# A graph kernel's third pass over the adjacency: resident rows moved to its end, two loads moved ahead of a branch, four sends moved to another queue

## The chip, the cores and the metric

The kernel is one launch on one core of a Trainium2 chip. The metric is the device time of the launch in microseconds (us). Three runs of the kernel before gave 1063.72, 1066.23 and 1070.17 us, a median of 1066.23. The profile is of another execution, which took 1063.12 us; its trace spans 1061.4 us from the first to the last instruction, and 1.7 us lie around that.

Names used below: TensorE (PE; its weight loads are shown as PEld), VectorE (DVE), ScalarE (ACT), GpSimd (POOL) and SyncE (SP). A name with a "q" behind it (SPq, ACTq) is the engine's sequencer, which issues DMAs, reads registers and branches.

## The reference

There are N = 2708 nodes with D = 128 features; `adj` is a sparse random matrix with weights, 2708 x 2708, of which the kernel gets the transpose as `adjT`. Four graph layers follow each other, each as `x = layernorm(x + layer(x, adj))`. The change lies in the second one:

```python
XW = jnp.matmul(X, W)
s_col = jnp.matmul(XW, a[0, :f])
s_row = jnp.matmul(XW, a[0, f:])
Z1 = jax.nn.leaky_relu(s_row[:, None] + s_col[None, :], negative_slope=0.01)
den = jnp.exp(Z1)
num = jnp.matmul(A, den)
att = jnp.where(num != 0, den / jnp.where(num != 0, num, 1.0), 0.0)
H = jnp.matmul(A, jnp.matmul(att, XW))
```

`num` would be a product of two full matrices. The kernel avoids that. `exp(leaky_relu(r + c))` is one of two products, `exp(r)exp(c)` or `exp(0.01r)exp(0.01c)`, depending on the sign of `r + c`. So for columns of `den` sorted by `c`, going from one block of columns to the next changes few rows' choice, and `num` of a block is `num` of the block before it plus the contribution of few rows of `adjT`.

## The kernel before

**The whole, in order of time.** A first pass over `adjT` makes the degrees and the first product of layer 0 (its last products start at 150 us). Then a search finds each node's four nearest nodes, and a second pass over `adjT` (`by_panels`, line 189, called at 1010) makes layer 0's output. The third pass, the subject here, runs from 442.4 us to 499.1 us of the trace. The loop over 44 steps (`block_layer`, line 1604) follows until about 724 us. Then three more passes by panels end layer 1 and make layers 2 and 3 (`two_layers`, line 1695).

**The third pass** (lines 1308 to 1447) does two things side by side.

The first is a product. `lc` holds for each node 22 weights: for each of the 11 chains of blocks, two sums are started (for the two forms of the exponential). `add_line(i, h, src)` (line 1335) multiplies row tile `i` of `adjT` (128 rows), half `h` of its 2708 columns (1354 columns), by `lc[:, i, :]`. Since only 32 columns of weights are used, it is four products side by side, one per quarter of the half row, each into 32 partitions of one PSUM bank, `banks[h]`. There are 21 full row tiles and one of 20 rows. Tiles 0 to 15 have to be loaded again: 32 half rows of 693,248 bytes, which `lines` (line 1022) lists, half 0 first; `line(n)` (line 1412) does the next n of them. Tiles 16 to 20 lie on the chip, in `res`, since the first pass: `own_line(n)` (line 1421) does the next n of these 10 half rows. `add_last_rows(h)` adds the 20 last rows. When a half's rows are all added, `end_half(h)` (line 1354) has ACT copy `banks[h]` to `heads` and ACT's queue send `heads` in four DMAs to the tile `carry`, which holds the two starting sums of each block.

The half rows are loaded by `load_line` (line 1033) on SP's queue into 11 places, `berths`: six in `ring`, three in `more`, two in `y_place`. The first 11 are loaded ahead. Each place is used again: `follows` (line 1026) says which half row is loaded when another has been read, and `line` issues that load. Half row 20 goes to the place of 11, 21 to that of 12, up to 28 to that of 19; then 29, 30 and 31 go to the places of 24, 25 and 26. Half rows 20 to 23 lie in the four places that are, put together, the first two thirds of `ring`.

The second thing is a sort, in between. It makes the order of the columns (`in_rank_order`, four parts, `ranks_known`), and then for each block the list of up to 126 rows to be fetched (`in_list_order`, four parts). Behind these come the row numbers `slot_i` and the weights `lw` (`listed`; six groups of `weights`, of which DVE makes four and ACT two).

What order TensorE, VectorE and ScalarE do all of this in is written out by hand, as the list `turns` (line 1429). SP and POOL take their instructions in the order in which the scheduler of the build puts them. On SP that is, behind the loads: three loads of the 20 last rows into `res` (line 1441), a read of `flag` into a register (line 1512), the branch (line 1773), the loop's carry rows.

**The branch** (line 1773) chooses between the loop by blocks and a dense way out, by the largest count in a list. Each engine reads `flag` and branches for itself.

**The loop** (line 1652) takes blocks two by two: 22 steps for each half of the columns. `load(i)` (line 1494) fetches for step i, per block, up to 126 half rows by an indirect DMA of POOL, and on SP two rows of `carry` into partitions 126 and 127 of the same place (line 1505). It uses one of three places in `ring`; step 0's is half row 20's and 21's, step 1's is half row 22's and 23's, step 2's is that of half rows 29 and 30. `find_num` multiplies by `lw`, `find_inv` has ACT do a logarithm and an exponential, `mix_1` to `mix_3` are DVE's. `keep(i)` sends two rows of the error term of each of the step's blocks on SP to `carry` for a later block. `add(i)` multiplies by `xws` into `hacc`. Loads run two steps ahead: `load(0)` and `load(1)` stand first behind the branch (lines 1647 and 1648), `load(i + 2)` first in step i.

Of the kernel before, what the change touches and what calls it, by code (L numbers as in the profile page):

```python
# [16 lines left out]
P = 128  # L17
# [4 lines left out]
KC = 126  # L22
CH = 4
# [29 lines left out]
def kernel(  # L53
# [999 lines left out]

    with tc.tile_pool(name="rank", bufs=1) as rank:
# [297 lines left out]
        HEADS = 96  # L1352

        def end_half(h):

            if not carries:
                carries.append(big.tile([P, NQ * P], F32, tag="y", name="carry"))
            tot = heads[:, h * span : (h + 1) * span]
            nc.scalar.copy(tot[:, : edges[4] - edges[3]], banks[h][:, : edges[4] - edges[3]])
            nc.scalar.copy(tot[:64, edges[4] - edges[3] :], banks[h][:64, edges[4] - edges[3] : span])  # L1360
            for g in range(4):
                w = edges[g + 1] - edges[g]
                nc.scalar.dma_start(
                    carries[0][HEADS : HEADS + 2 * NCH, h * HALF + edges[g] : h * HALF + edges[g + 1]],
                    tot[32 * g : 32 * g + 2 * NCH, :w],
                )
# [45 lines left out]
        def line(n):  # L1412
            for _ in range(n):
                at = loaded[0]
                loaded[0] += 1
                i, h = lines[at]
                add_line(i, h, line_at(at), last=at == 2 * S - 1)
                if at in follows:
                    load_line(follows[at])

        def own_line(n):
            for _ in range(n):
                h, i = divmod(held[0], FULL - S)
                held[0] += 1
                add_line(S + i, h, res[:, i, h * HALF : (h + 1) * HALF], last=held[0] == FULL - S)
# [4 lines left out]
            (line, 4), (blocks_of_edges,), (line, 7), (own_line, 2), (last_xw,), (in_rank_order, 0), (line, 2),  # L1430
            (in_rank_order, 1), (line, 2), (in_rank_order, 2), (count_lone,), (line, 2), (counts,), (line, 1),
            (add_last_rows, 0), (own_line, 3), (line, 2), (ranks_known,), (line, 1), (own_line, 1), (in_list_order, 0),
            (line, 1), (in_list_order, 1), (in_list_order, 2), (line, 1), (own_line, 1), (in_list_order, 3),
            (line, 1), (add_last_rows, 1), (next_weights,), (own_line, 1), (next_weights,), (line, 1), (next_weights,),
            (own_line, 1), (next_weights,), (line, 1), (next_weights,), (own_line, 1), (line, 1), (next_weights,),
            (line, 5),
# [3 lines left out]
        for c in range(C):  # L1440
            nc.sync.dma_start(res[few(c), FULL - S, cols[c]], adjT[FULL * P :, cols[c]])
# [3 lines left out]
        xws, lw = work["xws"], work["lw"]  # L1445
        order.close()
# [35 lines left out]
    adj_half = adjT.rearrange("n (h k) -> (n h) k", h=2)  # L1482
# [3 lines left out]

    def block(s):

        return s % NCH * CH + s // NCH

    steps = [(h, q) for h in range(2) for q in range(NQ)]
    rows = {}

    def load(i):
        h, q = steps[i]
        rows[i] = strip(i).rearrange("p (n k) -> p n k", n=2)
        for n in range(2):
            nc.gpsimd.indirect_dma_start(  # L1498
                out=rows[i][:KC, n, :], out_offset=None, in_=adj_half[:, :],
                in_offset=bass.IndirectOffsetOnAxis(ap=slot_i[h][:KC, 2 * q + n : 2 * q + n + 1], axis=0),  # L1500
                bounds_check=2 * N - 1, oob_is_err=False,
            )
            b = block(2 * q + n)
            at = 2 * b if b % CH else HEADS + b // CH * 2
            nc.sync.dma_start(rows[i][KC : KC + 2, n, :], carry[at : at + 2, h * HALF : (h + 1) * HALF])
# [98 lines left out]
    def block_layer():  # L1604
        with (
# [40 lines left out]
            with tc.manual_schedule(engines={e.engine for e in engines}):  # L1646
                load(0)
                load(1)
# [166 lines left out]
```

## Time and profile before

| stretch of the trace, us | what | PE busy | granted PE clock | DMA engines' busy share |
|---|---|---|---|---|
| 442.4 to 490.8 | third pass, half rows 0 to 29 | 47.30 of 48.40 | 0.99 | 0.84 |
| 490.8 to 499.1 | third pass, half rows 30 and 31 | 2.25 of 8.30 | 0.75 | 0.81 |
| 499.1 to 505.7 | to the loop's first logarithm | 3.66 of 6.60 | 0.53 | 0.30 |
| 505.7 to 519.0 | the loop's first steps | 10.33 of 13.30 | 1.00 | 0.49 |
| 519.0 to 723.8 | the rest of the loop | 204.09 of 204.80 | 1.00 | 0.55 |
| 0 to 1061.4 | the trace; the execution took 1063.12 | 984.6 (93%) | 0.97 | |

Each row gives PE's busy time in a stretch, the share of full speed that its clock was granted and how busy the 16 DMA engines were. Where PE's busy time equals the stretch, PE is what sets the pace; where it falls short, something else ends PE's waits. In such a profile a wait is put down to the event that came last before the waiting instruction began. Where the view names SP's line 1811 for a wait of PE, the two only ended at the same moment; what ended both is worked out below.

### The profile page before, as it was taken

Reading aid. Unit: us, or ns where it says so; the run is one execution under the profiler, and the core shown is the slowest. Engines: PE = TensorE matmul, PEld = TensorE weight load, DVE = VectorE, ACT = ScalarE, POOL = GpSimd, SP = SyncE. Lnnn points to the kernel's source line nnn. Section 1 sums busy time; section 2 is a strip of 40 time slices with the busy share of each in tenths; the row PEclk is TensorE's granted clock in tenths of the full one; section 3 lists DMA queues with packets and bytes.
Section 4 is the critical chain, followed back from the end, with each engine's and each line's share of the span. In section 5 each row is a group of like instructions: output and inputs, shape, how many; then the busy total and the mean of one; then the engine's idle time right before and its main releaser. Section 6 shows DMA issues by size and latency. Waiting matters only on the chain.

```text
span 1061.4 us, 11655 instructions
## 1 busy us (share of the span) xinstructions
PE 984.6 (93%) x3773; PEld 482.9 (45%) x3773; DVE 637.0 (60%) x1358; ACT 331.5 (31%) x609; POOL 275.1 (26%) x339
## 2 busy tenths in 40 slices
PE   0898999999998998796899999999999999999996
PEld 0346544444444556562333333334445544564444
DVE  5985438999944577862899999994121121222222
ACT  0000126555501245402767776762010100010000
POOL 4000000000477673023788534430121100000000
PEclk9989999999998998698999999999999999999998
DMA  9999340000185666696455555556665957484652
GB/s 339 373 342 270 109 157 1 0 1 1 32 279 183 221 182 201 224 359 200 118 167 152 149 146 157 142 163 215 219 193 169 308 168 219 145 276 149 227 170 72
DMA packets 102001, 191.00 MB, mean 180 GB/s; under 512 B 14022, under 2 KB 43342, under 8 KB 101930
## 3 DMA queue, kind: packets, MB, share of 16 engines
q1 hardware_dynamic: 83764, 152.22, 43.5%
q0 software_dynamic: 17728, 37.62, 12.8%
q8 instruction: 32, 0.52, 0.2%
q10 hardware_dynamic: 438, 0.31, 0.1%
q14 instruction: 39, 0.32, 0.1%
HBM read 214.80 MB, written 4.16 MB: 206 GB/s over the span
## 4 chain that ended last, share of the span: by engine, by line
PE 48%; DMA 1%; DVE 1%; ACT 1%; issue 1%; POOL 0%; POOLq 0%; DVEq 0%
PE acc L204 28%; PE num L1619 9%; PE hacc L1477 9%; PE mis L285 1%; DMA ring<-carry 1%; DMA ring<-in_adjT,slot_i 0%; PE mis L1750 0%; DVE inv L1466 0%; DVE err L1462 0%; ACT gb L234 0%; PE mis L1716 0%; DVE inv L1469 0%; PE mis L1746 0%; ACT inv L1452 0%; POOL rstd L253 0%
## 5 line engine op out<-in xcount | busy, mean ns | idle before, releaser
L1498 POOL DMA_INDIRECT ring<-in_adjT,slot_i x88 | 104.4, 1187 | 95.9 <-PE num L1619 67.0
L1619 PE MATMUL num<-ring,lw 128*64 128x512 f32 (+1 forms) x528 | 113.7, 557 | 6.1 <-DMA ring<-carry 3.8
L1477 PE MATMUL hacc<-inv,xws 128*128 128x512 f32 (+1 forms) x264 | 111.7, 559 | 0.6 <-ACT inv L1455 0.3
L699 PE MATMUL acc<-zT,z 128*128 128x512 f32 (+2 forms) x252 | 102.2, 552 | 0.0
L1452 ACT ACTIVATE inv<-num,plain 128x1024 f32<-128x1024 f32 x88 | 80.6, 916 | 57.6 <-PE num L1619 41.4
L253 POOL TENSOR_TENSOR rstd<-rstd,minus_half 128x4 f32<-128x4 f32 (+1 forms) x18 | 17.3, 960 | 313.5 <-DVE rstd L252 313.5
L234 ACT COPY gb<-acc 128x512 f32<-128x512 f32 (+2 forms) x18 | 9.6, 535 | 251.1 <-PE acc L204 251.1
L1462 DVE TENSOR_TENSOR err<-inv,num 128x1024 f32<-128x1024 f32 x88 | 74.6, 856 | 21.0 <-ACT inv L1455 19.7
L700 ACT COPY key<-acc 128x512 f32<-128x512 f32 (+2 forms) x126 | 67.1, 535 | 55.1 <-issue 27.9
L204 PE MATMUL acc<-ring,y 128*128 128x512 f32 (+2 forms) x192 | 82.0, 558 | 0.5 <-issue 0.5
L1477 PEld LDWEIGHTS hacc<-inv,xws 128*128 128x128 f32 x264 | 46.5, 189 | 77.6 <-issue 34.2
L729 POOL DMA_INDIRECT got<-y_rows,where x66 | 71.5, 1083 | 26.6 <-DVE near_sum L742 8.9
L204 PE MATMUL acc<-ring,xs 128*128 128x512 f32 (+2 forms) x192 | 78.1, 550 | 0.0
L1469 DVE SCALAR_TENSOR_TENSOR inv<-gb,g_inv,inv 128x1024 f32<-128x1024 f32 x88 | 77.2, 917 | 0.1
L204 PE MATMUL acc<-ring,carry 128*128 128x512 f32 (+2 forms) x192 | 74.5, 542 | 0.0
L204 PE MATMUL acc<-ring,m_rows 128*128 128x512 f32 (+2 forms) x192 | 74.3, 542 | 0.0
L1466 DVE SCALAR_TENSOR_TENSOR inv<-err,inv 128x1024 f32<-128x1024 f32 x88 | 72.3, 861 | 0.1
L575 POOL TENSOR_TENSOR slot_e<-near,sim 128x44 f32<-128x44 f32 (+2 forms) x3 | 0.7, 241 | 267.3 <-DVE d2inv L603 265.2
L699 PEld LDWEIGHTS acc<-zT,z 128*128 128x128 f32 x252 | 45.8, 190 | 50.4 <-issue 45.0
L1455 ACT ACTIVATE inv<-inv 128x1024 f32<-128x1024 f32 x88 | 67.6, 768 | 2.8
L1619 PEld LDWEIGHTS num<-ring,lw 128*64 128x64 f32 x528 | 37.4, 138 | 65.0 <-issue 47.5
L701 DVE MAX8 near<-key 128x8 f32<-128x2708 f32 x21 | 62.3, 2965 | 2.7 <-ACT key L700 2.7
(376 smaller groups left out, 1370.0 us busy)
## 6 DMA issues: line engine op xcount, KB each, us to landing
ring<-in_adjT SPq DMA_DIRECT2D x74, 1024.0 KB
ring<-in_adjT SPq DMA_DIRECT2D x20, 677.0 KB
ring<-in_adjT SPq DMA_DIRECT2D x17, 768.0 KB
part<-in_adjT SPq DMA_DIRECT2D x12, 1024.0 KB
ring<-in_adjT SPq DMA_DIRECT2D x17, 552.0 KB
more<-in_adjT SPq DMA_DIRECT2D x10, 677.0 KB
res<-in_adjT SPq DMA_DIRECT2D x4, 1280.0 KB
part<-in_adjT SPq DMA_DIRECT2D x3, 768.0 KB
```

Of the source, the lines that this page charges most:

```text
L204: nc.tensor.matmul(accs[c][: lhsT.shape[-1], :w], lhsT=lhsT, rhs=src, start=start, stop=stop)
L699: nc.tensor.matmul(pks[c][:p, : cw[c]], lhsT=z2[:, :p], rhs=zT[:, cs], start=False, stop=True)
L700: nc.scalar.copy(key[:p, cs], pks[c][:p, : cw[c]])
L729: nc.gpsimd.indirect_dma_start(out=got[:p, :], out_offset=None, in_=y2_rows[:, :], in_offset=bass.IndirectOffsetOnAxis(ap=where[:p, t, k : ...
L1452: nc.scalar.activation(inv, num[:, :w], AF.Ln, scale=plain[:, 0:1], bias=plain[:, 1:2])
L1455: nc.scalar.activation(inv, inv, AF.Exp, scale=-1.0)
L1462: nc.vector.tensor_mul(err, inv, num[:, :w])
L1466: nc.vector.scalar_tensor_tensor(inv, err, 2.0, inv, op0=ALU.subtract, op1=ALU.mult)
L1469: nc.vector.scalar_tensor_tensor(inv, gb[:, col : col + w], g_inv[:, q : q + 1], inv, op0=ALU.max, op1=ALU.mult)
L1477: nc.tensor.matmul(haccs[:, o:e], lhsT=xws[:, q, :], rhs=inv[:, o:e], start=(q == 0), stop=(q == NQ - 1))
L1498: nc.gpsimd.indirect_dma_start(out=rows[i][:KC, n, :], out_offset=None, in_=adj_half[:, :], in_offset=bass.IndirectOffsetOnAxis(ap=slot_i[ ...
L1619: nc.tensor.matmul(num[n * (BJ + 2) : (n + 1) * (BJ + 2), o:e], lhsT=lw[:, 2 * q + n, :], rhs=rows[i][:, n, c0 + o : c0 + e], start=True, ...
```

## The change

It consists of four edits.

1. `turns` is written anew. Most `own_line` steps move back: before, they came as 2, 3, 1, 1, 1, 1, 1; now as 4, 1, 1, 1, 1, 2, the last two being the end of the list. `line` steps move forward in turn; the `add_last_rows(1)` goes from the middle to just before the last two own lines. The accumulation of each half now ends with an own line (`last` in `own_line`) and no longer with the last loaded half row.
2. `load` and what it needs (`block`, `steps`, `rows`, `adj_half`, `HEADS`) are defined before the third pass, and `load(0)` and `load(1)` are called at its end. Their DMAs thus stand before the read of `flag` and the branch on POOL (four indirect DMAs) and on SP (four carry row DMAs, ahead of the sends below).
3. `end_half` sends only half 0 on ACT's queue. Half 1's four sends are issued on SP by `send_half`, behind the carry rows.
4. The loads of the 20 last rows (line 1441) stand behind these sends.

In the built kernels the same numbers of matmuls, DMAs and vector operations stand on the engines; SP has four sends more and ACT four fewer.

```diff
+    def load(i):
+        h, q = steps[i]
+        rows[i] = strip(i).rearrange("p (n k) -> p n k", n=2)
+        for n in range(2):
+            nc.gpsimd.indirect_dma_start(
+                out=rows[i][:KC, n, :], out_offset=None, in_=adj_half[:, :],
...
+            b = block(2 * q + n)
+            at = 2 * b if b % CH else HEADS + b // CH * 2
+            nc.sync.dma_start(rows[i][KC : KC + 2, n, :], carry[at : at + 2, h * HALF : (h + 1) * HALF])
...
             nc.scalar.copy(tot[:64, edges[4] - edges[3] :], banks[h][:64, edges[4] - edges[3] : span])
+            if h == 0:
+                send_half(h, tot, nc.scalar)
+
+        def send_half(h, tot, queue):
+
             for g in range(4):
                 w = edges[g + 1] - edges[g]
-                nc.scalar.dma_start(
+                queue.dma_start(
                     carries[0][HEADS : HEADS + 2 * NCH, h * HALF + edges[g] : h * HALF + edges[g + 1]],
                     tot[32 * g : 32 * g + 2 * NCH, :w],
                 )
...
-                add_line(i, h, line_at(at), last=at == 2 * S - 1)
+                add_line(i, h, line_at(at))
...
-                add_line(S + i, h, res[:, i, h * HALF : (h + 1) * HALF], last=held[0] == FULL - S)
+                add_line(S + i, h, res[:, i, h * HALF : (h + 1) * HALF], last=held[0] % (FULL - S) == 0)
...
         turns = [
-            (line, 4), (blocks_of_edges,), (line, 7), (own_line, 2), (last_xw,), (in_rank_order, 0), (line, 2),
-            (in_rank_order, 1), (line, 2), (in_rank_order, 2), (count_lone,), (line, 2), (counts,), (line, 1),
-            (add_last_rows, 0), (own_line, 3), (line, 2), (ranks_known,), (line, 1), (own_line, 1), (in_list_order, 0),
-            (line, 1), (in_list_order, 1), (in_list_order, 2), (line, 1), (own_line, 1), (in_list_order, 3),
-            (line, 1), (add_last_rows, 1), (next_weights,), (own_line, 1), (next_weights,), (line, 1), (next_weights,),
+            (line, 4), (blocks_of_edges,), (line, 7), (last_xw,), (in_rank_order, 0), (line, 3),
+            (in_rank_order, 1), (line, 3), (in_rank_order, 2), (count_lone,), (line, 2), (counts,), (line, 3),
+            (add_last_rows, 0), (own_line, 4), (ranks_known,), (line, 2), (own_line, 1), (in_list_order, 0),
+            (line, 1), (in_list_order, 1), (in_list_order, 2), (line, 2), (in_list_order, 3),
+            (next_weights,), (own_line, 1), (next_weights,), (line, 2), (next_weights,),
             (own_line, 1), (next_weights,), (line, 1), (next_weights,), (own_line, 1), (line, 1), (next_weights,),
-            (line, 5),
+            (line, 1), (add_last_rows, 1), (own_line, 2),
         ]
         for f, *args in turns:
             f(*args)
-        for c in range(C):
-            nc.sync.dma_start(res[few(c), FULL - S, cols[c]], adjT[FULL * P :, cols[c]])
         end_half(1)
...
+        load(0)
+        load(1)
+        send_half(1, heads[:, span:], nc.sync)
+        for c in range(C):
+            nc.sync.dma_start(res[few(c), FULL - S, cols[c]], adjT[FULL * P :, cols[c]])
...
             with tc.manual_schedule(engines={e.engine for e in engines}):
-                load(0)
-                load(1)
                 late_q = list(range(SOON, NQ))
```

More of the change, by code (lines that the diff above doesn't have):

```diff
@@ L1052, in fetch_xw, with block @@
         )
+    adj_half = adjT.rearrange("n (h k) -> (n h) k", h=2)
+    HEADS = 96
+    def block(s):
+        return s % NCH * CH + s // NCH
+    steps = [(h, q) for h in range(2) for q in range(NQ)]
+    rows = {}
+    def load(i):
[4 more added lines that the diff above has]
+                out=rows[i][:KC, n, :], out_offset=None, in_=adj_half[:, :],
+                in_offset=bass.IndirectOffsetOnAxis(ap=slot_i[h][:KC, 2 * q + n : 2 * q + n + 1], axis=0),
+                bounds_check=2 * N - 1, oob_is_err=False,
+            )
+            b = block(2 * q + n)
+            at = 2 * b if b % CH else HEADS + b // CH * 2
+            nc.sync.dma_start(rows[i][KC : KC + 2, n, :], carry[at : at + 2, h * HALF : (h + 1) * HALF])
     with tc.tile_pool(name="rank", bufs=1) as rank:
@@ L1350, in add_last_rows @@
                 )
-        HEADS = 96
         def end_half(h):
@@ L1481 @@
     psum.close()
-    adj_half = adjT.rearrange("n (h k) -> (n h) k", h=2)
     WIDE = 2 * CW
@@ L1485 @@
     assert 0 < NARROW <= CW
[L1487 to L1505, printed above, removed]
     m_rows = row_tile("m_rows").rearrange("p (t d) -> p t d", d=D)
```

## The prediction

> **What bounds the kernel now.** I read the busy times by stretch first, to find where TensorE is not the bound, then TensorE's timeline there, then SP's and ACT's timelines, SP's waits and the chain of waits. Around the third pass the stretches are (columns: busy us and count of PE, PEld, DVE, ACT, POOL; clock; DMA share; GB/s):
>
> ```profile
> 442.40:490.80 48.40, 47.30 (x489) 25.17 (x488) 32.57 (x76) 7.90 (x29) 14.75 (x14) 0.99 0.84 307
> 490.80:499.10 8.30, 2.25 (x16) 0.36 (x16) 0.11 (x1) 0.00 (x0) 2.56 (x3) 0.75 0.81 216
> 499.10:505.70 6.60, 3.66 (x11) 2.26 (x13) 0.00 (x0) 1.77 (x3) 0.56 (x1) 0.53 0.30 83
> ```
>
> PE is full to 490.8, then has 15 us in which it works for 5.9. TensorE's timeline shows the first half of that hole:
>
> ```profile
> 490.03 0.75 PE L1337 MATMUL acc<-ring,lc 128*32 128x339 f32 x8
> 494.48 0.90 PE L1337 MATMUL acc<-ring,lc 128*32 128x339 f32 x8 [3.71 <-DMA ring<-in_adjT]
> 497.69 1.35 PE L1337 MATMUL acc<-more,lc 128*32 128x339 f32 x8 [2.31 <-SPq L1811]
> ```
>
> These are half rows 29, 30 and 31: PE waits for the last two loads. (The second wait is labelled with an SP event; the trace has half row 31 landing at 497.65.) Why they are late stands on SP's queue, in its timeline and its own waits:
>
> ```profile
> 484.21 2.90 SPq L1035 DMA_DIRECT2D ring<-in_adjT  x2
> 488.64 0.33 SPq L1035 DMA_DIRECT2D more<-in_adjT  x1
> 489.02 1.34 SPq L1441 DMA_DIRECT2D res<-in_adjT  x3
> 497.74 6.61 SPq L1505 DMA_DIRECT2D ring<-carry  x6
> ```
>
> ```profile
> SPq L1035 <- DMA carry<-heads: 6.5, 1, 6.5
> ...
> SPq L1811 <- SPq L1811: 8.6, 2, 6.3
> ```
>
> Half rows 29, 30, 31 are issued at 484.21, 486.78, 488.64, when PE has read 24, 25, 26, and share the DMA engines with the four indirect loads of the loop's steps 0 and 1, which POOL issues from 481.88 on. Half row 26 had stood until 473.13 behind ACT's first send of half 0 (the 6.5). The 6.3 is SP behind its branch: its first carry row uses the semaphore of half row 31 and waits for that landing. So the carry rows leave at 497.74, and the chain of waits goes on with them:
>
> ```profile
> 497.74 4.17 DMA ring<-carry
> 501.90 0.14 issue
> 502.04 1.75 PE num L1619 x3
> ...
> 505.74 1.22 ACT inv L1452
> ```
>
> ACT's timeline is not far behind:
>
> ```profile
> 499.12 0.44 ACT L1359 COPY heads<-acc 128x338 f32<-128x338 f32 x1 [10.60 <-PE acc L1337]
> 499.45 0.15 ACT L1360 COPY heads<-acc 64x1 f32<-64x1 f32 x1
> 499.64 3.23 ACTq L1363 DMA_DIRECT2D carry<-heads  x4
> 503.88 1.28 ACT L1609 ACT_TABLE_LOAD   x1 [4.27 <-SPq L1811]
> ```
>
> From 519 us PE is full again (204.09 of 204.80), so what counts is the time of the first logarithm, 505.74, from which the loop's start-up follows.
>
> **What the Trainium skill says.** "DMA: Bandwidth & Descriptors", section "Anatomy of one DMA": about 2 us fixed plus bytes over 436 GB/s. For a half row that makes 2.0 + 693,248 / 436,000 = 3.6 us; half row 26, alone on the engines, took 473.13 to 476.71, 3.58. The same page, "Queues, rings and completion order": an engine goes round between the queues that have work. Half rows 30 and 31, beside the indirect loads, took 6.3 and 9.0 us. "TensorE: Matmul & The Clock Gate", Part 1: after an idle window of about 3.4 us the array gets half its clock. The trace has 0.5 from 495.0 to 505.2, behind the 3.71 us wait. "Advanced Engine Details and Errata", "Control Flow Timing": compare-and-branch 108 ns; the five here took 51 to 95. The branch itself is thus no price.
>
> **The change, part by part.** Duration sums are against the profiled execution (span 1061.4, 1.7 around it, 1063.12). It lies 3.1 below the median of the runs, 1066.23; I take the difference over to the median.
>
> *The order of the lines.* The work of PE is the same. From 442.42 to 490.78 it did all but half rows 30 and 31, at 0.57 each (two in 1.28 with the change of weights): with the data there it ends at 490.8 + 1.1 = 491.9. Laying the new list out with the durations of the same steps in the old one gives 491.8, some changes of weights fewer. Does the data come? Half rows 11 to 25 landed some 1.67 us apart, the DMA engines full: 447.8 for 11, 457.0 for 16, 461.1 for 18, 466.2 for 21, 472.9 for 25. In the new list PE wants 16 at 458.8, 18 at 461.6, 21 at 466.6, 25 at 478.5. So the slack is 0.4 at the closest (18, 21). Moving own lines away takes PE's cover there; if a load is 1 us later, PE loses 0.6 at once. I take 0, with 1 for the range. Half row 26 no longer stands behind ACT's send: in the changed kernel's instruction order those sends come behind the issues of 27 and 28. 24, 25, 26 are read at 475.0, 478.5, 479.1, so 29, 30, 31 leave by 479.8, before the first indirect load. With 3.6 us each, or 6.3 where an indirect load is beside it, they land by 486; PE wants 29 at 486.1 and 31 at 489. The list chain pays: `ranks_known` ends at 471.5 for 471.0 and the last list part at 481.1 for 480.1, but POOL's memset and six gathers (10.4 us) set the indirect loads: 482.4 instead of 481.88, the fourth landing near 491, before it is wanted (493). Own lines hide that half microsecond; without them it would be 0.5. Sum: 499.04 - 491.8 = 7.2 gained.
>
> *Loads ahead of the branch.* POOL gains nothing: it had already branched at 476.85. SP issues the four carry rows behind half row 31, from 479.9, 0.62 each (the four issues from 497.74 to 500.53); half 0's sends have landed by then (ACT issues them from 474, 0.8 each). So they land some 8 us before PE ends, and the wait of 4.17 is gone. What is late next is ACT. `find_num(0)` needs the banks, hence ACT's copies: 491.85 + 0.6 = 492.5. Then 8 products, 1.8 us at full clock by the loop's own rate: 494.4. PE's idle time is under 1 us there, so I count full clock (half clock: 496.2).
>
> *Half 1's sends on SP.* ACT loses 4 x 0.81 us. (Half 0's, still on ACT, now come behind `g_col`, which waited 3.4 for them; nothing wants `g_col` before 481, so that is worth nothing.) But its first logarithm writes over the place of `heads`: in the changed kernel's instruction order it waits for the semaphores of all four sends. They begin on SP at 492.55. SP's DMAs between tiles took 0.56 plus 0.05; ACT's of this shape 0.776. Between 0.33 (SP's shortest) and 0.78 I take 0.62; the fourth begins at 492.55 + 3 x 0.67 = 494.55 and lands 1.9 later (on ACT: 502.08 to 504.01): 496.45. That is later than 494.4 or 496.2, so the logarithm starts at 496.4 (495.6 to 497.0), 4.6 behind PE's end where it was 6.7: 2.1 gained. ACT's table load (1.28) is done by 494.
>
> *Behind the sends on SP*: three loads of last rows (1.24; they overwrite what `add_last_rows(1)` reads, which is now done at 490.5, before SP comes to them), the flag and the branch (1.0), then step 2's carry rows at 497.8 and 498.5, formerly 2.7 us before the logarithm, now 1.4 behind it. They land 3.5 to 4.5 later, at 502 to 503; `find_num(2)` could begin 4.8 behind the logarithm, at 501.2. It waits 0.8 to 1.8. Behind it PE has 5.1 us of work until step 3's rows, which come 10.9 behind the logarithm (516.66 - 505.74), a slack of 1.1; so 0 to 0.7 stays, I take 0.2. Step 3's rows stand behind `keep(0)`, which waits for DVE 3.6 behind the logarithm; SP is free by then.
>
> *The power on POOL* (line 253, 4.02 us) stood before step 7's indirect loads and made PE wait 0.43 at 537.7. In the new order it stands before step 3's, which have 4 us to spare: 0.4 gained.
>
> Sum: 7.2 + 2.1 - 0.2 + 0.4 = 9.5. The profile's 1063.1 becomes 1053.6; the median 1066.2 becomes 1056.7.
>
> **The rivals.**
> *A, the forecast*: 1056.7; with its bounds (lines 1 later, sends 0.8 less or 0.6 more, start-up 0 to 0.7, clock) 1055 to 1059.5, and 2 us of spread between runs on either side.
> *B, SP becomes the bound of the start-up*: sends at 0.78, slow landings (4.5) and a PE that falls to half clock while it waits for `find_num(2)` (3.4 us at half rate, 1.7 more). Then 9.5 - 0.6 - 0.5 - 1.7 - 1.0 = 5.7 is left: 1060.5. For it: SP has 7 us of issues in a row. Against: the chain's slack.
> *C, the loads stay late*: the change doesn't do what it says. PE reads 24 to 26 only 7 to 9 us earlier; if indirect loads overtake 30 and 31 as before (9.0 us each), 31 lands at 489 and PE hardly waits; only with two lines late by 5 us more is the gain down to 4: 1062. For it: they overlapped in the old trace. Against: three lines leave before the first indirect load.
> *D, slower*: the loop starts in another phase. Now DVE runs at 4.76 us a step and gets ahead, and PE sets 4.89. `num` for the narrow piece has one buffer, so PE's next product waits for DVE's `err`. If the start leaves DVE just behind PE, each of the 42 steps pays that handover, say 0.3 us: 12.6, against 9.5 gained: 1069.3. It decides from 0.23 us a step on. Against it: DVE's step is shorter, so it catches up within a few steps.
>
> **How the numbers follow.** A 0.72, B 0.12, C 0.10, D 0.06. The predicted time is A's, 1056.7. The range leaves out D and the outer part of A and C: 1052 to 1062.5. About 0.5%, 5.3 us, is what a measurement tells from no change here, so the line for faster is 1060.9. A lies below it nearly whole (0.69), B half (0.06), C by 0.03: faster 0.78; the same 0.16; slower 0.06.
>
> **What would show it.** No wait of PE on half rows 29 to 31, the third pass's last product at 491 to 493; carry rows of steps 0 and 1 issued by SP near 480; the first logarithm at 495.5 to 497.5, released by a send; `find_num(2)` waiting 1 to 2 us on a carry row; PE full from some 508 on. I am wrong if PE waits for half rows 17 to 21, if the logarithm waits beyond 499, or if loop steps grow beyond 4.89.

## The result, and the profile after

The kernel after took 1054.32 us (median of 4 runs, 1052.89 to 1056.23), the kernel before on the same chip 1064.97 (4 runs, 1063.60 to 1070.17): a ratio of 0.9876, 95% interval 0.9846 to 0.9906. The forecast was 1056.7. The profiled execution took 1053.01 with a span of 1051.3.

The experiments ran on four other chips, where the two kernels take 15 to 25 us more and their runs spread over 9 to 20 us. There the gain was not always to be had: 0.9999 (0.9974 to 1.0024) on one, 0.9931 (0.9911 to 0.9950) on another. Why is the main part of what follows.

The stretches of the kernel after, with the columns of those of before:

```profile
441.40:490.50 49.10, 48.06 (x485) 25.64 (x485) 31.62 (x74) 7.90 (x29) 15.79 (x15) 0.95 0.88 329
490.50:492.60 2.10, 2.01 (x28) 0.53 (x24) 1.09 (x3) 0.02 (x1) 1.32 (x2) 1.00 0.62 186
492.60:498.10 5.50, 4.31 (x20) 2.45 (x20) 0.00 (x0) 1.78 (x4) 5.26 (x3) 1.00 0.44 108
498.10:512.40 14.30, 10.26 (x31) 4.06 (x31) 11.19 (x15) 10.34 (x14) 8.64 (x8) 0.76 0.46 129
```

The hole of 15 us behind the half rows is gone; what is left of it is mainly one wait of 4.67 us. The granted clock is 1.00 from 490.5 to 498.1, where it was 0.75 and 0.53, but 0.95 in the pass, where it was 0.99, and 0.76 in the loop's first steps, where it was 1.00. TensorE's timeline (start, us, line, operation, count, and what ended the idle time before it):

```profile
453.61 3.35 PE L1360 MATMUL acc<-ring,lc 128*32 128x339 f32 x24
...
458.35 1.91 PE L1360 MATMUL acc<-ring,lc 128*32 128x339 f32 x24
...
489.76 0.78 PE L1360 MATMUL acc<-more,lc 128*32 128x339 f32 x8
...
493.17 4.31 PE L1627 MATMUL num<-ring,lw 128*64 128x512 f32 x20 [0.66 <-ACT heads L1381]
502.14 5.11 PE L1627 MATMUL num<-ring,lw 128*64 128x330 f32 x12 [4.67 <-DVE err L1491]
507.18 2.81 PE L1506 MATMUL hacc<-inv,xws 128*128 128x512 f32 x6
509.92 2.50 PE L1627 MATMUL num<-ring,lw 128*64 128x330 f32 x12
```

No wait on half rows is left; 489.76 is half row 31. The two groups of 24 at 453.61 and 458.35 are the same work, three half rows each, the first mostly at half clock. At 502.14 stands one wait of 4.67 us, and the group behind it takes 5.11 where its twin at 509.92 takes 2.50. SP's timeline, and ACT's:

```profile
476.50 3.93 SPq L1035 DMA_DIRECT2D ring<-in_adjT  x2
480.67 1.17 SPq L1035 DMA_DIRECT2D more<-in_adjT  x1
482.53 2.64 SPq L1075 DMA_DIRECT2D ring<-carry  x4
493.10 3.29 SPq L1389 DMA_DIRECT2D carry<-heads  x4
496.43 1.26 SPq L1474 DMA_DIRECT2D res<-in_adjT  x3
498.86 1.41 SPq L1075 DMA_DIRECT2D ring<-carry  x2
```

```profile
492.58 0.44 ACT L1380 COPY heads<-acc 128x338 f32<-128x338 f32 x1 [3.17 <-PE acc L1360]
...
493.23 1.28 ACT L1617 ACT_TABLE_LOAD   x1 [0.15 <-issue]
498.08 1.20 ACT L1481 ACTIVATE inv<-num,plain 128x1024 f32<-128x1024 f32 x1 [3.57 <-DMA res<-in_adjT]
```

The half rows and carry rows leave early, as forecast. The first logarithm starts at 498.08, after a wait of 3.57. The view puts that wait down to the loads of the last rows (`res`); experiments below show that it was for the four sends.

To compare kernels I cut each trace at five points that all share: the pass's first product, ACT's copy of half 1's sums, the first logarithm, a fixed product of step 1, one of step 6, one of step 17. The change in one pair of traces then is: pass 56.70 to 51.16, copy to logarithm 6.62 to 5.50, logarithm to step 1 13.67 to 14.80, steps 1 to 6 the same 16.62, steps 6 to 17 64.13 to 62.28. In all 157.75 to 150.37, 7.38 less. The rest of the 10.1 us between the two executions lies outside: 1.0 ahead of the pass and 1.7 near 966 us, where before's trace has 3.4 us of half clock and after's has none. From step 17 on the loop is alike in both.

All the traces in these cuts (us; "half clock" is what began 10 to 13 us into the pass, and its length):

| kernel | pass | copy to log | log to step 1 | steps 6 to 17 | half clock |
|---|---|---|---|---|---|
| before | 56.70 | 6.62 | 13.67 | 64.13 | none |
| before, another chip (r_before) | 56.31 | 6.70 | 12.87 | 67.45 | none |
| after | 51.16 | 5.50 | 14.80 | 62.28 | 3.4 |
| after again (r_after) | 60.30 | 5.32 | 14.53 | 62.55 | 20.5 |
| after again (r_after2) | 52.97 | 5.41 | 13.99 | 63.44 | 3.4 |
| e1_order | 55.55 | 6.19 | 12.90 | 66.85 | 10.2 |
| e2_moves | 55.43 | 5.65 | 12.94 | 63.91 | none |
| e3_act_sends | 60.30 | 6.41 | 14.04 | 63.72 | 20.5 |
| e4_pow_early | 61.87 | 6.34 | 22.33 | 65.82 | 10.2 |
| e5_pow_late | 55.48 | 5.30 | 13.71 | 71.99 | 10.2 |
| e5b_pow_late | 55.53 | 6.24 | 14.87 | 64.36 | 10.2 |
| e6_heads | 52.88 | 2.71 | 13.66 | 64.92 | 3.4 |
| e7_heads_load2 | 55.49 | 2.71 | 12.49 | 67.59 | 10.2 |
| e9_fill | 51.23 | 6.00 | 14.26 | 62.13 | none |
| e10_all | 51.61 | 2.71 | 12.55 | 65.27 | none |
| e11_inter | 51.70 | 5.58 | 13.81 | 63.47 | none |
| e12_swap | 55.85 | 6.24 | 13.06 | 69.83 | none |
| e13_early | 59.57 | 6.06 | 13.03 | 65.65 | 6.8 |
| e14_pow_pass | 50.10 | 2.72 | 14.29 | 63.49 | none |
| e15_res_late | 53.72 | 5.24 | 14.20 | 62.18 | 3.4 |

Steps 1 to 6, which the table leaves out, take 16.62 us in all traces but e6_heads (16.66), e10_all (17.02), e7_heads_load2 (17.30) and e15_res_late (17.79). Each row is one execution. What lies outside the cuts is not the change's: the part ahead of the pass, the same code in all, took 452.0 us in r_after's trace and 463.5 in r_after2's.

### The profile page after: what moved, and what is told of

Read it like the earlier page. It is cut to its first block, busy times and chain, and to the rows that moved or that the text cites. A ratio compares the mean times of both kernels' runs of the same rounds, so it can differ in the third digit from the quotient of the medians.

```text
span 1051.3 us, 11657 instructions
## 1 busy us (share of the span) xinstructions
PE 981.7 (93%) x3773; PEld 481.5 (46%) x3773; DVE 637.8 (61%) x1358; ACT 331.6 (32%) x609; POOL 265.4 (25%) x339
## 4 chain that ended last, share of the span: by engine, by line
PE 72%; DVE 16%; DMA 6%; ACT 2%; issue 2%; POOL 1%; SPq 1%; POOLq 0%; DVEq 0%; ACTq 0%
PE acc L204 34%; PE hacc L1506 10%; PE num L1627 10%; PE acc L428 7%; DVE where L702 6%; DVE near L701 5%; DMA res<-in_adjT 3%; PE acc L1360 3%; DMA got<-y_rows,where 1%; PE mis L285 1%; PE acc L699 1%; DMA part<-in_adjT 1%; DVE both L483 1%; POOL ring L125 1%; PE mis L1090 1%
## 5 line engine op out<-in xcount | busy, mean ns | idle before, releaser
L1068 POOL DMA_INDIRECT ring<-in_adjT,slot_i x88 | 93.7, 1065 | 96.2 <-PE num L1627 77.4
L701 DVE MAX8 near<-key 128x8 f32<-128x2708 f32 x21 | 62.3, 2965 | 2.7 <-ACT key L700 2.7
```

The source lines that it names most:

```text
L701: nc.vector.max(near[:p, t, :], key[:p])
L1068: nc.gpsimd.indirect_dma_start(out=rows[i][:KC, n, :], out_offset=None, in_=adj_half[:, :], in_offset=bass.IndirectOffsetOnAxis(ap=slot_i[ ...
```

## The experiments

Ratios are to the kernel before on the same chip, with 95% intervals.

### The parts of the change

**e1_order**: only the new `turns` and `last`, in the kernel before.

> The kernel before with the new order of lines alone; loads and sends stay where they were. Theory (the order's worth is the waits for half rows 30 and 31, 7.2 us, less what a half clock takes; the rest comes from elsewhere): no wait of TensorE on half rows, the pass 5.5 to 7.2 us shorter. But the loads of the last rows (L1474 in the kernel after) now stand behind the last rows' late product, so SyncE passes the branch only near 492.5 and the carry rows of steps 0 and 1 land near 496 to 498: TensorE waits about 4 us for them as before. GpSimd's power stays ahead of step 7's loads and costs its 1.8. Time 1058 to 1060. Rival (the order alone makes the whole change): 1054 to 1055.

Ratio 0.9991 (0.9969 to 1.0013): the order alone gained nothing that can be measured. The time expected, 1058 to 1060, was about 0.5 per cent below the kernel before. The waits on half rows are gone, but the pass is 1.1 us shorter and not 5.5, since 10.2 us of it ran at half clock. SP's timeline shows the loads of the last rows in the way, as expected:

```profile
499.55 8.23 SPq L1441 DMA_DIRECT2D res<-in_adjT  x3
508.00 6.82 SPq L1505 DMA_DIRECT2D ring<-carry  x6
```

The three take 8.23 us because the last of them waits for the late `add_last_rows(1)`. TensorE then waited 1.50 us with no releaser named and 1.79 for the carry rows, less than the 4 expected. Yet copy to step 1 took 19.09, no more than the 20.30 of the kernel after.

**e2_moves**: the kernel after with the old `turns` and `last`.

> The kernel after with the old order of lines: only the loads ahead of the branch and half 1's sends on SyncE. Theory: the pass ends as late as before (waits on half rows 30 and 31, about 4 and 3 us), the wait for carry rows (4.2 us) goes but the first logarithm is bound by the sends, 1 to 2 us sooner; the power now stands ahead of step 3's loads, 1.8 gained. Sum 2 to 4: 1061 to 1063. Rival (the moves are worth nothing without the order, and the power's place is worth the 0.4 of the visible wait): 1063.5 to 1065.

Ratio 0.9953 (0.9934 to 0.9973), more than expected. Copy to step 1 is 18.59 us (before 20.29, and 19.57 in r_before), steps 6 to 17 are 63.91.

**e3_act_sends**: `send_half(1, ..., nc.scalar)` in the kernel after.

> The kernel after with half 1's four sends left on ScalarE. Theory (the first logarithm waits for the sends and ScalarE's own queue): its start comes 6 to 7 us after the copy instead of 5.50, the loop 0.5 to 1.5 us later: 1054.8 to 1056. Rival (SyncE behind its sends, with step 2's carry rows, is what bounds the start): SyncE is 3.3 us freer, step 2's rows land 3 us sooner, and the time is 1052 to 1054.

Ratio 0.9979 (0.9958 to 0.9999). Its trace has the same half clock as r_after, so the two compare: copy to logarithm 6.41 against 5.32, as expected, copy to step 1 20.45 against 19.85. The queue is worth some 0.6 us by this one pair; the kernel after's own three traces spread over 0.9 there (19.40 to 20.30), and the times don't tell the two kernels apart.

**r_after** and **r_before**: the kernels unchanged, on other chips.

> The kernel after, unchanged, as the partner of the next three on their chip. Theory (the change is worth 5.5 in the pass, 1.1 at the logarithm, 1.85 from the power's place, less 1.1 at the start of the loop, and a half clock that sets in 10 us into the pass takes part of it back): 3 to 8 us below the kernel before of the same chip, with the half clock again near 10 to 11 us after the pass's first product. Rival (the half clock in the pass is chance): no half clock there, and 9 us below.

> The kernel before, unchanged, for a trace of it beside the next three. Theory (the half clock in the pass belongs to the new order): as in the first trace, full clock from the pass's first microseconds to the waits on half rows, the logarithm some 63 us after the pass's first product, the stretch from there to step 17 some 158 us in all. Rival (that chip grants less clock in any case): a half clock in the pass here too.

r_after 0.9999 (0.9974 to 1.0024); r_before 0.9997 (0.9970 to 1.0023), with full clock in the pass. r_after's pass took 60.30 us, 3.6 longer than that of before, with no wait on half rows. Its timeline, from 10 us into the pass:

```profile
461.85 2.45 PE L1201 MATMUL js<-val_q,hot_in 128*128 128x44 f32 x12
464.23 3.61 PE L1360 MATMUL acc<-ring,lc 128*32 128x339 f32 x24
467.77 2.79 PE L1201 MATMUL js<-val_q,hot_in 128*128 128x44 f32 x12
470.49 3.61 PE L1360 MATMUL acc<-ring,lc 128*32 128x339 f32 x24
```

Each group takes 1.6 to 1.9 times as long as the same group at full clock (1.53 and 1.91 in e9_fill, below). So a half clock within a busy stretch takes the gain: with the new order, 10.2 us of it make the pass 55.5 long (e1, e5, e5b, e7), 20.5 us make it 60.3, where it is 51.2 without (e9_fill). The cuts agree with the times: their sum is 159.95 in r_before, 159.32 in r_after and 152.43 in r_after2, so 0.6 and 7.5 us less; the medians on the two chips are 0.1 and 6.2 us below the kernel before. How often each length of half clock comes among the runs isn't known, since one execution of each was traced.

### What sets the half clock

**e9_fill**: two own lines go back ahead of the transposes.

```diff
-            (line, 4), (blocks_of_edges,), (line, 7), (last_xw,), (in_rank_order, 0), (line, 3),
+            (line, 4), (blocks_of_edges,), (line, 7), (own_line, 2), (last_xw,), (in_rank_order, 0), (line, 3),
...
-            (add_last_rows, 0), (own_line, 4), (ranks_known,), (line, 2), (own_line, 1), (in_list_order, 0),
+            (add_last_rows, 0), (own_line, 2), (ranks_known,), (line, 2), (own_line, 1), (in_list_order, 0),
```

> The kernel after with two lines of rows on the chip put back ahead of the three transposes (turn last_xw), and taken from the later place; all else the same. So far the half clock came 10 to 12 us into the pass in all four traces with the new order and in neither of the two with the old one. Theory (the new order brings the thin stretch of the transposes earlier, and that brings the half clock): full clock through the pass, 1.7 us or more sooner than the kernel after. Rival (chance, or the line count alone): the half clock is there as often, and the time is the same.

Ratio 0.9942 (0.9918 to 0.9965), on r_after's chip: 1073.50 to r_after's 1079.71. Full clock through the pass:

```profile
472.60 1.53 PE L1201 MATMUL js<-val_q,hot_in 128*128 128x44 f32 x12
474.07 1.91 PE L1360 MATMUL acc<-ring,lc 128*32 128x339 f32 x24
```

**e11_inter**: the transposes and products of `last_xw` spread between lines.

```diff
-            (line, 4), (blocks_of_edges,), (line, 7), (last_xw,), (in_rank_order, 0), (line, 3),
+            (line, 4), (blocks_of_edges,), (line, 6), (last_x, 0), (line, 1), (last_w, 0), (last_x, 1), (line, 1),
+            (last_w, 1), (last_x, 2), (line, 1), (last_w, 2), (line, 1), (in_rank_order, 0),
...
```

> The kernel after with the three transposes and products of the last rows (last_xw) spread between four lines, so that no 3.4 us of the pass hold only transposes and the thin products that follow them. Theory (a stretch of about 3.4 us with little matrix work sets the half clock, and it was 4.5 us long): full clock through the pass whatever the phase, TensorE's three waits of 1.03 us in all gone: the logarithm at 52 to 53.5 us after the pass's first product, 1 us or so below e9_fill and 6 below the kernel after of the same chip. Rival (e9_fill was luck of the phase or chance): a half clock in the pass here in some form, the time near the kernel after's.

Ratio 0.9870 (0.9819 to 0.9921). No half clock in the pass. The pass took 51.70, 0.5 longer than e9_fill's and not 1 us less, and the logarithm came 57.3 us into the pass, not 52 to 53.5: a wait of 0.47 for a half row and some 2 us in which TensorE stood near 498 us with nothing that the profile names took the gain back. e9_fill and r_after show the latter too, the first trace of after doesn't; I can't say what it is. The kernel after wasn't run on this chip.

**e12_swap** and **e13_early**: the same two own lines in the order of before, moved behind the transposes, or behind these and the first thin products.

```diff
-            ... (own_line, 2), (last_xw,), (in_rank_order, 0), ...
+            ... (last_xw,), (own_line, 2), (in_rank_order, 0), ...      e12_swap
+            ... (last_xw,), (in_rank_order, 0), (own_line, 2), ...      e13_early
```

> The kernel before with one swap in its order: the two lines of rows on the chip go between the transposes (last_xw) and the thin products that follow them, instead of ahead of both. Theory (a half clock needs some 3.4 us that hold only thin work; ahead of the swap the thin stretch is 4.5 us long and its place against the clock's steps decides): the stretch is cut into 3 and 1.5 us, no half clock in the first 50 us of the pass; the same as the kernel before or up to 2 us less. Rival (thin work early in the pass is what matters, the sooner the worse): half clock near 10 us into the pass, 4 to 9 us slower.

> The kernel before with those two lines moved behind both the transposes and the first thin products: the thin stretch stays 4.5 us long and comes 1.25 us sooner, as in the changed kernel, and nothing else of the change is there. Theory: half clock near 10 us into the pass for 3.4 us or more; since the pass then waits for half rows 30 and 31 anyway, part of that is hidden: the pass 0 to 4 us longer, the time 0 to 5 us more than before. Rival (the half clock comes from the lines on loaded rows that follow each other, or from chance): full clock, the same time as before.

e12_swap 0.9999 (0.9983 to 1.0015), no half clock; e13_early 1.0012 (0.9993 to 1.0032), half clock from 10.0 us into the pass for 6.8. A group of thin products and 16 of the pass's own behind it, in e12_swap's timeline and in e13_early's:

```profile
467.81 1.54 PE L1178 MATMUL js<-val_q,hot_in 128*128 128x44 f32 x12
469.28 1.34 PE L1337 MATMUL acc<-ring,lc 128*32 128x339 f32 x16
```

```profile
469.21 2.64 PE L1178 MATMUL js<-val_q,hot_in 128*128 128x44 f32 x12
471.77 2.48 PE L1337 MATMUL acc<-res,lc 128*32 128x339 f32 x16
```

In both traces full clock came at the same point, 0.2 us ahead of the pass's first product. So one move of two lines sets the half clock, without any other part of the change and at the same phase.

**What decides.** In all 20 traces the granted clock changes only on a grid of 3.41 us. It comes to full between 0.2 us ahead of the pass's first product and 2.9 us behind it, and where it drops again 10 to 13 us into the pass, it does so exactly three steps later. In the twelve traces with the drop, the step just before it held 0 to 0.47 us of the pass's own products on half rows; the rest was transposes, the products on them and thin products (columns 128 and 44), and 0.55 to 1.04 us of waits for ScalarE's copies between them. In the eight traces without, that step held 0.54 us or more of products on half rows (before 0.54, e9_fill 0.58). Whether it gets that half microsecond is decided by the phase of the grid and by where the thin stretch of 4.5 us begins: 6.9 to 7.6 us into the pass with the new order in nine traces of ten, 8.1 to 8.8 with the old. All ten traces of the new order as written dropped. The old one isn't safe: of four, e4_pow_early came out with 0.47, and dropped. TensorE's busy time alone does not decide: in the step ahead of r_after's drop it was busy for 2.37 of 3.41 us, in the same step of before, without a drop, for 2.37 as well.

```profile
458.85:462.26 3.41, 2.37 (x17) 1.46 (x13) 3.38 (x7) 1.30 (x6) 1.17 (x2) 1.00 1.00 415
```

```profile
450.63:454.04 3.41, 2.37 (x17) 1.05 (x10) 3.31 (x8) 1.04 (x5) 0.78 (x2) 1.00 1.02 418
```

The half microsecond is a limit for this one step, whose other work is nearly the same in all kernels but e10, e11 and e14. It is no general one. e1_order's step from 477.41 held 0.43 us of products on half rows and kept full clock; TensorE worked for all of its 3.41 us, mostly on the counting products (bf16, up to 484 columns). e2_moves's step from 506.90, among the waits for half rows 30 and 31, held 0.78 us of them and nothing else, and dropped. So it is neither these products nor the busy time alone, but some sum of a step's work to which a transpose or a thin product adds less than a product on a half row. How much each adds, these runs don't show.

The Trainium skill, "TensorE: Matmul & The Clock Gate", Part 1, has the half clock follow an idle window of about 3.4 us, and says that the windows run freely. The grid agrees; but here windows in which TensorE worked for 2.37 to 2.86 of 3.41 us were followed by it too. How long it lasted went with the phase. In the ten traces of the new order it was 20.5 us where full clock had come with the pass's first product (two traces), 10.2 where it had come 0.1 to 0.3 us later (four), and 3.4 where it had come 1.3 to 2.9 us later (four). What brings full clock back isn't shown: r_after's last step at half clock, from 479.33, held 0.26 us of products on half rows.

### The start of the loop

**e7_heads_load2**, **e6_heads**, **e15_res_late**: the sums' place, step 2's loads and the loads of the last rows; first all three, then the first and the last alone. e6_heads:

```diff
-            tot = heads[:, h * span : (h + 1) * span]
+            if h:
+                carries.append(row_tile("sums_1"))
+            tot = carries[1][:, :span] if h else heads
```

> The kernel after with half 1's sums copied to a row tile, so that the loop's first tile no longer lies over what is sent; step 2's loads ahead of the branch and the sends; the three loads of the last rows (L1474) moved to step 6. Theory (the first logarithm waits for the sends through that place alone): it starts when its operand is there, some 2.5 us after the copy instead of 5.50; TensorE's idle 4.67 before step 1 shrinks to about 1.5, too short for the half clock; 3 to 4.5 us sooner than the kernel after. Rival (ScalarE's table load and branch, or step 2's rows, hold the start anyway): under 1 us.

> The kernel after with half 1's sums copied to a row tile instead of heads, and nothing else: e7_heads_load2 had changed three things at once. Theory (the first logarithm waits for the four sends because its tile lies over heads): it starts 2.7 us after the copy, as in e7_heads_load2. What it wins is partly lost again, since step 2's carry rows still come behind the sends, the last rows' loads and the branch: TensorE then waits for these some 2 us; 0.5 to 2 us gained. Rival (what ends the logarithm's wait is the loads of the last rows, which the view names as the releaser): it stays at 5.3 to 5.6.

> The kernel after with the three loads of the last rows moved from before the branch to the last but one step of the loop; heads stays where it is. Theory (the sends' landings hold the logarithm): it starts 5.0 to 5.5 us after the copy as before; SyncE reaches step 2's carry rows 1.3 us sooner, nothing else moves: 0 to 0.5 us gained. Rival (the loads of the last rows hold it): it starts 3 us or so after the copy.

Ratios 0.9950 (0.9926 to 0.9975), 0.9895 (0.9847 to 0.9942), 0.9922 (0.9887 to 0.9956). With the sums elsewhere the logarithm starts 2.71 us after the copy; with only the loads of the last rows moved it stays at 5.24. So it is the place, and the view's name for the releaser, `res`, was wrong. e15_res_late lost elsewhere what was not expected: steps 1 to 6 took 17.79 us for 16.62, 1.10 of it a wait of TensorE that the view puts down to ScalarE's exponential. ACT's timeline of e6_heads:

```profile
512.76 0.44 ACT L1382 COPY sums<-acc 128x338 f32<-128x338 f32 x1 [2.92 <-PE acc L1360]
...
515.47 1.20 ACT L1483 ACTIVATE inv<-num,plain 128x1024 f32<-128x1024 f32 x1 [0.78 <-PE num L1629]
```

TensorE's wait before step 1 fell from 4.67 to 1.88, the clock stayed full, and copy to step 1 took 16.37 us, 3.0 less than in r_after2, whose half clock in the pass was as long. The kernel after wasn't run on the chip of e6_heads and e15_res_late, so their times don't say what the place is worth. e6_heads then waits 0.82 for step 2's carry rows; e7_heads_load2, which has them early, does not. But e7_heads_load2 gave its gain back at step 9: its six loads of the last rows, put into step 6, kept SP for 2.29 us, and the carry rows came late:

```profile
562.38 1.04 PE L1628 MATMUL num<-ring,lw 128*64 128x512 f32 x2 [1.63 <-DMA ring<-carry]
564.20 3.23 PE L1628 MATMUL num<-ring,lw 128*64 128x512 f32 x6 [0.78 <-DMA ring<-carry]
```

### The power on GpSimd

The power is the element-wise `deg + eps` to the -0.5 of line 253, which GpSimd works out for the layers behind the loop. None of the four edits moves it; with them the build puts it ahead of step 3's loads, where before it stood ahead of step 7's. **e5_pow_late**, **e5b_pow_late**: the power back in step 5, ahead of step 7's loads. **e4_pow_early**: early, in the kernel before. e5b_pow_late's edit:

```diff
+                    if i == 0:
+                        nc.vector.tensor_scalar_add(dinv, deg, DEG_EPS)
+                    if i == 5:
+                        nc.gpsimd.tensor_tensor(dinv, dinv, minus_half[:, :T], op=ALU.pow)
```

> The kernel after with GpSimd's power put back ahead of step 7's indirect loads (step 5 of the loop). Theory (the 1.85 us between 517 and 600 is the power's place): a step at 530 to 550 with longer products, 1.5 to 2 us lost: 1055.8 to 1056.4. Rival 1 (the prediction: only the visible wait of 0.43): 1054.7. Rival 2 (the 1.85 us is another stretch's luck, such as the half clock): no step there, 1054.3.

> The kernel after with GpSimd's power back ahead of step 7's indirect loads, and its addition on VectorE left first, as it stands in both kernels (the first attempt, e5_pow_late, also made the power wait 5.8 us for that addition). Theory (a power of 4 us puts GpSimd's queue behind; the loads of the next steps come late one after another, until its 1 us of slack per step has made it up): 1.5 to 2.5 us lost between steps 6 and 10. Rival (the visible wait alone): 0.4.

> The kernel before with GpSimd's power alone moved, from ahead of step 7's loads to ahead of step 3's, where the kernel after has it. Theory (the power puts GpSimd's queue behind for some steps, early it falls into the slow start): the steps of 5 to 10 at one pace, 1.5 to 2.5 us gained: ratio near 0.998. Rival (the visible wait of 0.43 only): no difference that can be measured, steps of 2.6 to 2.8 us around step 8 as before.

e5_pow_late 1.0040 (1.0017 to 1.0063) and e4_pow_early 1.0059 (1.0036 to 1.0081) tell little of the power itself: I had moved VectorE's addition along with it, so that GpSimd waited 5.77 and 14.01 us for VectorE with its loads queued behind. e5b_pow_late, without that fault, has 1.0009 (0.9986 to 1.0032), and r_after on its chip 0.9999: the times don't tell the two apart. In the traces steps 6 to 17 took 64.36 for r_after's 62.55: 1.8 lost, within the theory. e5b_pow_late's GpSimd timeline:

```profile
541.30 4.02 POOL L1663 TENSOR_TENSOR dinv<-dinv,minus_half 128x22 f32<-128x22 f32 x1
545.53 1.88 POOL L1069 DMA_INDIRECT ring<-in_adjT,slot_i  x1 [0.22 <-issue]
547.72 1.06 POOL L1069 DMA_INDIRECT ring<-in_adjT,slot_i  x1 [0.30 <-issue]
549.09 1.55 POOL L1049 DMA_INDIRECT xws<-xw_rows,row_j  x1 [0.30 <-issue]
550.94 1.32 POOL L1069 DMA_INDIRECT ring<-in_adjT,slot_i  x1 [0.30 <-issue]
```

and that of the kernel after at the same loads, step 7's and the first of step 8's:

```profile
520.78 1.04 POOL L1068 DMA_INDIRECT ring<-in_adjT,slot_i  x1 [0.98 <-PE num L1627]
522.12 1.05 POOL L1068 DMA_INDIRECT ring<-in_adjT,slot_i  x1 [0.30 <-issue]
523.48 1.21 POOL L1048 DMA_INDIRECT xws<-xw_rows,row_j  x1 [0.30 <-issue]
525.67 1.04 POOL L1068 DMA_INDIRECT ring<-in_adjT,slot_i  x1 [0.98 <-PE num L1627]
```

In the kernel after GpSimd waits 0.98 us per step for TensorE; that is its slack. Behind the power it has no such wait up to 600 us, and three of TensorE's next `num` groups take 2.98 to 3.42 us for 2.50. The power stands early in eleven traces without another cause of delay there (all but e4 and e7): 62.1 to 65.3 us, mean 63.4; late in six (before, r_before, e1, e12, e13, e5b): 64.1 to 69.8, mean 66.4. These sums hold other waits too, and e12's 3.4 us of half clock. Without its waits TensorE was busy in these steps for 62.1 to 63.5 us in the eleven, 62.3 in e4, and 63.7 to 66.9 in the six.

### All of it

**e10_all**: e11_inter's order, e7_heads_load2's place and early loads, the last rows' loads after the last step's. **e14_pow_pass**: that, and the power in the third pass.

> e11_inter with e7_heads_load2's place for the sums and its early loads of step 2; the loads of the last rows now after the last step's loads instead of step 6, where they put SyncE behind. Theory (the two gains are apart, and the loss of 5 us at step 9 of e7_heads_load2 came from those loads): 3 to 5 us below e11_inter, 1.2 per cent or more below the kernel before. Rival (SyncE or GpSimd is too late for the earlier loop, and gives the start's gain back): the same as e11_inter.

> e10_all with GpSimd's power moved once more, from the loop's start into the third pass, where GpSimd has nothing queued that TensorE waits for soon. Theory (the power leaves GpSimd behind for seven steps whatever step it stands in; e10_all lost 3 us between steps 6 and 17 against e9_fill to that): steps 6 to 17 in 62 us instead of 65.3, 2 to 4 us below e10_all's distance from before: ratio 0.981 to 0.983. Rival (SyncE's carry rows are what is late there): steps 6 to 17 in 65 us again, the ratio of e10_all, 0.984.

> The kernel after, unchanged, once more as the partner of these. Theory: half clock 10 us into the pass for 3.4 to 20 us, the time from 0.2 per cent above to 1.2 per cent below the kernel before, by how long it lasts on this chip. Rival (the chip of the first comparison or the one of r_after was the exception): no half clock, 0.7 to 1 per cent below.

e10_all 0.9844 (0.9792 to 0.9895): below the kernel before as expected, but 1.7 us below e11_inter's median and not 3 to 5. e14_pow_pass 0.9883 (0.9839 to 0.9926) on a chip where r_after2 has 0.9931 (0.9911 to 0.9950); 1069.78 us against 1076.25. e14_pow_pass thus beats the kernel before there, and by its median the kernel after too (the two intervals overlap a little), and its cuts sum to 147.22 us, 3.2 less than the best trace of the kernel after. Steps 6 to 17 took 63.49 in it, not 62: a wait of 1.18 us of TensorE with no releaser named stands in them. GpSimd waits a microsecond per step again, which in e10_all it did not for six steps. The ratio expected, 0.981 to 0.983, was not reached, and the intervals of e10_all and e14_pow_pass overlap: that the power's last move pays is seen in the traces, not in the times.

## Where the prediction was wrong, and where right

The time fell near the forecast, 1054.32 for 1056.7, and the waits on half rows 30 and 31 went, as said. But the step with the largest term failed, three others were mis-sized, and that the total came so near is in part luck. The sum of 9.5 us was 7.4 in the traces; 2.7 us of the difference between the two profiled executions have nothing to do with the change. By medians the gain was 10.65. Of the 2.4 us to the forecast, 1.3 is the base: the kernel before has 1064.97 over four runs, and the forecast started from 1066.23. On two other chips the gain was 0.1 and 6.2 us.

- *Order of the lines, 7.2 gained: the step that failed.* 5.5 in the first pair. The loads behaved: no wait on any half row, 31 landing at 488.38 and read at 489.76. What failed is the clock. The step laid the new list out "with the durations of the same steps in the old one", all of them at full clock, and half clock was thought of only as a follower of a long wait. Moving two own lines from ahead of the transposes left a stretch of thin work and short waits, and the half clock behind it took 1.7 us (24 products 3.35 for 1.91, and part of the group ahead). On other chips it lasted longer and took 4.3 to 9.1, most or more than all of what the order gains (some 5 us there, e9_fill against r_before). This is the term that decides whether the change pays.
- *Loads ahead of the branch, 4.17 us of wait gone*: the wait went, as written. But it was only moved: between copy and step 1 the kernel before took 20.29 and 19.57 us, the kernel after 20.30, 19.85 and 19.40.
- *Half 1's sends, 2.1 gained*: 1.12. The mechanism, the place of `heads`, is shown by e6_heads and e15_res_late. Mis-sized was the issue on SP: 0.62 taken, 0.73 to 0.84 measured, about the upper bound that I had set aside. Against ACT's queue it is some 0.6 (e3_act_sends, one pair).
- *SP behind the sends, 0.2 lost*: 1.13 lost. TensorE waited there for DVE's `err` (502.14: the narrow piece of step 1's `num`, with `find_num(2)` right behind it), and not for carry rows. The early first products left it one wait of 4.67 us where it had two (3.00 and 1.83), and half clock followed from 500.9 to 507.8. Rival B had the half clock there at 1.7; it was counted as a rival and belonged in the forecast, since TensorE's next product waits for logarithm, exponential and `err` one after the other, 4.06 us from 498.08 to 502.14, in both kernels.
- *The power, 0.4 gained*: 1.85 in the pair, 3.0 by the means. The term counted the visible wait of TensorE. A queue with about 1 us of slack per step needs several steps to make up 4, and some of them run late. The traces show it; the times don't.

Two landings were misread: half row 26 took 4.3 us (473.13 to 477.46), not 3.58, and half row 30 took 7.7 (486.78 to 494.44), not 6.3. Both counts took in arrivals of ACT's earlier sends on the same semaphores. The estimate of 3.6 comes from the Trainium skill, "DMA: Bandwidth & Descriptors", section "Anatomy of one DMA", which gives its sum for DMAs issued from GpSimd; half row 26, issued from SyncE with two more right behind it, took 0.7 us more. In the changed kernel half row 31 landed 2.4 us later than forecast, still before it was wanted.

Rivals C and D did not come: half row 31 landed in time, and steps 1 to 6 take 16.62 us in both kernels.

## What to carry to other kernels

When a dense product is used as filler between thin products, moving it can cost more than its own time says: look for stretches of 3.4 us that would be left with thin work and short waits only, and keep some of the dense product in each. When a wait on the critical path is removed, follow the idle engine to its next wait, and add up the idle time in one piece. A long operation on a queue that feeds a loop is better priced by the queue's slack per step than by the one wait that can be seen.

## What the runs showed of the hardware

- A clock step with TensorE busy for 2.37 to 2.86 of 3.41 us, mostly on transposes and thin products, was followed by the half clock, as the nearly idle step from 507.93 in r_before was (0.14 us of work): 12 of 20 traces, all with at most 0.47 us of products on half rows in that step, none with 0.54 or more. In other steps other limits hold (0.43 without a drop, 0.78 with one).
- A DMA between tiles took SP longer to issue than a load: in the kernel after 0.73 to 0.84 us for the sends of 22 rows, 0.57 to 0.71 for two carry rows, against 0.33 for most half rows.
- The same kernels differ by chip: the kernel before took 1064.97 us on the first and 1079.49 to 1084.78 (medians) on the four others. Traces there reach the third pass 10 to 21 us later; why, I didn't try to find out.
- What stays open: TensorE's unnamed waits on the other chips, some 2 us 38 to 50 us into the pass in all traces of the new order there, and 1.0 to 1.2 in the loop in four.
